# A dummy GpSimd write after every gather, and distances written in place of their comparison

## The chip, the cores and the metric

The kernel runs on one core of a Trainium2 chip. Times are device microseconds of that core for one launch; the time of a kernel is the median of several runs without the profiler. A profile is a separate execution of the same program under the hardware profiler, and its span can differ from the timed runs. Engines: PE (TensorE, matrix products; PEld are its weight loads), DVE (VectorE), ACT (ScalarE), POOL (GpSimd, which here issues indirect DMAs and little else), SP (SyncE, which issues the plain DMAs).

## What is computed

For each of 16 graphs with 1024 nodes and 64 channels: normalize and clip the node features, drop some neighbours by their rank in the adjacency row, take three quantiles per channel over the neighbours that remain, and put the weighted sum through a small two-layer network.

```python
h = jnp.maximum(_layernorm(x, axis=-1), 0.0)
# in the layer, x is h:
neigh = (adj_ > 0) & ~eye
rank = jnp.cumsum(ni, axis=-1) - ni                    # ni = neigh as integers
skip = jnp.where(nb > T, (nb + K - 1) // K, 1)         # nb = neighbours per node, T = 10, K = 2
rem = neigh & (sk > 1) & (rank % sk == sk - 1) & mask[:, :, None]
rem = rem | jnp.swapaxes(rem, 1, 2)
vals = jnp.where(nd[..., None], x[:, None, :, :], jnp.inf)   # nd: neighbours kept
s = jnp.sort(vals, axis=2)
for tau, w in zip((0.25, 0.5, 0.75), (0.25, 0.5, 0.25)):
    ...                                                # v_lo, v_hi: s at floor/ceil of tau * (nv - 1)
    agg = agg + w * (v_lo + frac * (v_hi - v_lo))
out = x + agg
y = jax.nn.relu(out @ W1 + b1) @ W2 + b2
```

## The kernel before

The kernel makes a list of neighbours per node, gathers their feature rows from a table in DRAM, and sorts the gathered rows with a fixed network. `drop` computes a distance `dist` (is this neighbour's rank one that is dropped?) and compares it; `keep` makes the remaining adjacency; `order` sorts the nodes by their number of neighbours (`perm`); `collect` packs the lists (`idx`). The tiles `rem` and `perm` share one buffer (tag `wide`, `bufs=1`).

```python
    def drop(b):
        ...
        rem = wk.tile([P, NT, N], BF16, name="rem", tag="wide", bufs=1)
        rems[b] = rem
        for t in range(NT):                                    # NT = 8
            dist = wk.tile([P, N], F16, name="dist")           # two buffers
            for n in range(2):
                rk = psum.tile([P, HALF], F32, name="rk", tag="mx", bufs=3)
                nc.tensor.matmul(rk, cnt[:, ts], ...)          # L702
                for s in range(4):
                    nc.tensor.matmul(rk[:, s * P:(s + 1) * P], ne[:, 4 * n + s, ts], upper, ...)   # L707
                nc.scalar.activation(dist[:, n * HALF:(n + 1) * HALF], rk, AF.Abs, bias=bias[:, t:t + 1])   # L711
            nc.vector.tensor_scalar(rem[:, t], dist, 1.0, half[:, t:t + 1], OP.add, OP.is_equal)   # L712
```

The gathers. A pair of batches has nodes in four classes by neighbours, each class with its own tile `g` (the first two, `g0` and `g1`, have two buffers, `g4` and `g6` one). Per batch there are 12 + 10 + 10 + 9 + 8 + 7 + 6 + 5 = 67 gathers, 1072 in all; each moves one row of 64 numbers to each of 128 partitions.

```python
CLASSES = (((0,), 13), ((1, 2, 3), 11), ((4, 5), 9), ((6, 7), 7))

    def fetch(m, classes=CLASSES, halves=(0, 1)):
        for tiles, slots in classes:
            lo, n = tiles[0], len(tiles)
            ...   # g = wk.tile(..., name=f"g{lo}", bufs=2 - lo // 4)
            for h in halves:
                nc.scalar.copy(g[:, slots - 1, :, h], owns[m][:, lo:lo + n, h])
                idx, tab = lists[2 * m + h], tables[2 * m + h]
                for k in tiles:
                    for s, slot in enumerate(order[:CAPS[k] - 1]):
                        at = PASSED[k] + s
                        nc.gpsimd.indirect_dma_start(          # L930
                            out=g[:, slot, k - lo, h], out_offset=None, in_=tab,
                            in_offset=bass.IndirectOffsetOnAxis(ap=idx[:, at:at + 1], axis=0),
                        )
```

`aggregate(m, o)` sorts and weighs a pair's tiles on VectorE (L961, L962 minima and maxima, L969 weights), first `g6` and `g4`, then asks for the next pair's `g4` and `g6`, then `g1` and `g0`. Nodes with many neighbours are treated in two groups of eight batches by `fetch_group` (L1100, 44 gathers, and L1104). The main loop weaves the preparation of the next pair between the results of this one:

```python
    for m in range(pairs + 1):                                 # pairs = 8
        if 0 < m < pairs:
            fetch(m, CLASSES[:1])
            ...                                                # a group's gathers, for two values of m
            fetch(m, CLASSES[1:2])
        ...
        side = chain(*(prepare(b) for b in (2 * m + 2, 2 * m + 3) if b < B))
        weave(chain(results(m - 1) if m else (), (1.0,)), 140.0 if m else 1.0, side, 85.0)
```

Instructions are placed on each engine's queue by a scheduler that respects the dependencies; `tc.keep_in_program_order` pins an instruction behind the one written before it on the same engine.

Of the kernel before, what the change touches and what calls it, by code (L numbers as in the profile page):

```python
# [28 lines left out]
F16 = mybir.dt.float16  # L29
BF16 = mybir.dt.bfloat16  # L30
FP8 = mybir.dt.float8e4
FP8W = mybir.dt.float8e5
I32 = mybir.dt.int32
# [6 lines left out]
P = 128  # L40
N = 1024
# [43 lines left out]
FP8_PARTS = (0, P, 2 * P, 3 * P, 4 * P, 4 * P + 17, 4 * P + 32)  # L85
# [449 lines left out]
def list_layer(  # L535
# [14 lines left out]
    nc = tc.nc  # L550
# [3 lines left out]
    cst = ctx.enter_context(tc.tile_pool(name="cst", bufs=1))  # L554
    wk = ctx.enter_context(tc.tile_pool(name="wk", bufs=2))
# [5 lines left out]
    def ask(b, t):  # L561
# [10 lines left out]
    ident16, ones16, minus16, before16, base, blocks, own2 = (  # L572
        kb[:, lo:hi] for lo, hi in zip(BF_PARTS, BF_PARTS[1:])
    )
    raw = wk.tile([P, FP8_PARTS[-1]], BF16, name="raw", tag="dist")
    nc.sync.dma_start(out=raw, in_=cbf[:, BF_AT:BF_AT + FP8_PARTS[-1]])
    rows_u8 = wk.tile([B * NT, P], U8, name="rows_u8", tag="rest", bufs=1)
    nc.sync.dma_start(out=rows_u8, in_=nodemask.rearrange("b (t p) -> (b t) p", p=P))
# [111 lines left out]
    def drop(b):  # L690

        ne = neT[b]
        bias, half = nbs[b]
        cnt = counts[b]
        rem = wk.tile([P, NT, N], BF16, name="rem", tag="wide", bufs=1)
        rems[b] = rem
        for t in range(NT):
            ts = slice(t * P, (t + 1) * P)
            dist = wk.tile([P, N], F16, name="dist")
            for n in range(2):  # L700
                rk = psum.tile([P, HALF], F32, name="rk", tag="mx", bufs=3)
                nc.tensor.matmul(  # L702
                    rk, cnt[:, ts], blocks[0:NT, 4 * n:4 * n + 4, None].to_broadcast([NT, 4, P]), start=True, stop=False,
                    skip_group_check=True,
                )
                for s in range(4):
                    nc.tensor.matmul(  # L707
                        rk[:, s * P:(s + 1) * P], ne[:, 4 * n + s, ts], upper, start=False, stop=(s == 3),
                        skip_group_check=True,
                    )  # L710
                nc.scalar.activation(dist[:, n * HALF:(n + 1) * HALF], rk, AF.Abs, bias=bias[:, t:t + 1])  # L711
            nc.vector.tensor_scalar(rem[:, t], dist, 1.0, half[:, t:t + 1], OP.add, OP.is_equal)  # L712
            yield 0.5
# [199 lines left out]
    pairs = B // 2  # L913
    gathered, groups = {}, {}

    def fetch(m, classes=CLASSES, halves=(0, 1)):

        for tiles, slots in classes:
            lo, n = tiles[0], len(tiles)
            held, order = PLANS[slots][:2]  # L920
            if (m, tiles) not in gathered:
                gathered[m, tiles] = wk.tile([P, held, n, 2, C], F32, name=f"g{lo}", bufs=2 - lo // 4)
            g = gathered[m, tiles]
# [7 lines that stand above are left out]
                            out=g[:, slot, k - lo, h], out_offset=None, in_=tab,  # L931
                            in_offset=bass.IndirectOffsetOnAxis(ap=idx[:, at:at + 1], axis=0),
                        )


    pause = cst.tile([P, 1], F32, name="pause")
# [61 lines left out]
    def aggregate(m, o):  # L998


        last = m == pairs - 1
        coef = coefs[m]
        for half in (0, 1) if last else (1, 0):
            acc = psum.tile([P, 4, 2, C], F32, name="acc", tag="agg", bufs=2)
            parts = CLASSES[2 * half:2 * half + 2][::1 if last else -1]
            for tiles, slots in parts:
                lo, n = tiles[0], len(tiles)
                nc.tensor.matmul(
                    acc[:, lo - 4 * half:lo - 4 * half + n], ident32, gathered[m, tiles][:, slots - 1],
                    start=((tiles, slots) == parts[0]), stop=False, skip_group_check=True,  # L1010
                )
            for tiles, slots in parts:
                lo, n = tiles[0], len(tiles)
                g = gathered.pop((m, tiles))
                plan = PLANS[slots]
                for k in tiles:
                    for slot in plan[1][CAPS[k] - 1:]:
                        nc.vector.memset(g[:, slot, k - lo], BIG)
                yield from sort(
                    g.rearrange("p s n h c -> p s (n h c)"), plan, window(tiles, slots)[0],  # L1020
                    lambda s, many: coef[:, s:s + many, lo:lo + n].rearrange("p s n h -> p s (n h)"),
                    acc[:, lo - 4 * half:lo - 4 * half + n],
                )
            if half and not last:
                fetch(m + 1, CLASSES[2:])
            terms(acc, [o[:, 4 * half:4 * half + 4, :, C * n:C * n + C] for n in range(3)])
# [145 lines left out]
    def prepare(b):  # L1172
        yield from both(drop(b), load(b + 1) if b + 1 < B else iter(()), normalize(b))
        yield from keep(b)
        yield from order(b)
        yield from collect(b)
# [28 lines left out]
    for _ in range(4):  # L1205
        next(ahead)
    late_constants()
    drain(both(ahead, drop(0), normalize(0)), keep(0), order(0), collect(0, ((0, 1), (1, NT))))
    fetch(0, halves=(0,))
    drain(load(1), prepare(1))  # L1210
    fetch(0, halves=(1,))
    for m in range(pairs + 1):
        if 0 < m < pairs:
# [92 lines left out]
@with_exitstack  # L1306
def quantile_graph_layer(
    ctx: ExitStack,
    tc: tile.TileContext,
    x: bass.AP,  # L1310
    adj: bass.AP,
    nodemask: bass.AP,
    W1: bass.AP,
    b1: bass.AP,
    W2: bass.AP,
    b2: bass.AP,
    cbf: bass.AP,
    cf32: bass.AP,
    ci32: bass.AP,
    out: bass.AP,  # L1320
):
    keep = ctx.enter_context(tc.tile_pool(name="keep", bufs=1))
    flag = keep.tile([1, 1], I32, name="flag")
    list_layer(tc, x, adj, nodemask, W1, b1, W2, b2, cbf, cf32, out, flag)
    full = tc.nc.values_load(flag[0:1, 0:1], min_val=0, max_val=1)
    with tc.If(full > 0):
        dense_layer(tc, x, adj, nodemask, W1, b1, W2, b2, cbf, cf32, ci32, out)
# [78 lines left out]
```

## Time and profile before

| | |
|---|---|
| time, median of 3 | 2034.06 us (2023.58 to 2036.27) |
| span under the profiler | 2713.0 us, mean granted TensorE clock 0.688 |
| gathers of `fetch` (L930) | 1072, mean 1.001 us each on POOL |
| sorting steps (L961, L962) | 408 each, 0.70 us each on DVE |
| `dist` (L711) | 256 on ACT, 0.69 us each |
| comparison (L712) | 128 on DVE, 0.49 us each |
| bytes moved | 130.12 MB, mean 48 GB/s over the profiled span |

A group of instructions in the profile is read as: line, engine, operation, tiles, count; busy time and mean of one; idle time of its engine just before, and what ended that idle time. "issue" is time in which an engine waited for nothing that the profile shows, "remote" or "an unknown queue" a wait whose end the profile can't assign to an instruction.

### The profile page before, as it was taken

The numbers are of one execution on the slowest core, as the hardware profiler recorded it, in microseconds if no ns is written. First come the engines' busy times: TensorE is split into PE (matmuls) and PEld (weight loads), VectorE is DVE, ScalarE is ACT, GpSimd is POOL, SyncE is SP. The second block draws the span as 40 slices with busy tenths as digits, with TensorE's granted clock in tenths as the row PEclk, the third lists the DMA queues.
The fourth block names the chain that finished last, engine by engine and source line by source line (L and its number), as shares of the span: only waits on it lengthen the run. The fifth ranks groups of instructions, "written<-read, shape, count | busy, mean of one in ns | idle before, by whom it ended". The sixth has DMA issues, their size and how long they took to land.

```text
span 2713.0 us, 25381 instructions
## 1 busy us (share of the span) xinstructions
PE 1377.2 (51%) x8367; PEld 737.9 (27%) x8385; DVE 1162.5 (43%) x3634; ACT 926.9 (34%) x2414; POOL 1128.6 (42%) x1129
## 2 busy tenths in 40 slices
PE   7227163433664655645564555643565665514435
PEld 3114132211332323322232333322332323202223
DVE  2202255232322752453523652466633554338692
ACT  6247243323552533243342544232341532100101
POOL 0630726353325454455525355445325345537100
PEclk7657576665776767766687767756677677656767
DMA  3232212021222231212212121222111211111000
GB/s 99 64 79 72 59 47 61 14 71 45 78 53 47 48 84 24 67 49 66 48 37 59 43 73 37 55 65 49 53 42 24 62 23 19 30 22 22 20 0 11
DMA packets 152591, 130.12 MB, mean 48 GB/s; under 512 B 117570, under 2 KB 118082, under 8 KB 152450
## 3 DMA queue, kind: packets, MB, share of 16 engines
q1 hardware_dynamic: 116482, 91.51, 12.1%
q0 software_dynamic: 35968, 36.90, 8.0%
q8 instruction: 68, 1.11, 0.2%
q14 instruction: 73, 0.60, 0.1%
HBM read 112.78 MB, written 13.81 MB: 47 GB/s over the span
## 4 chain that ended last, share of the span: by engine, by line
PE 37%; another core or an unknown queue 33%; issue 11%; ACT 10%; DVE 8%; DMA 1%; POOL 0%; SPq 0%; POOLq 0%; DVEq 0%; ACTq 0%
PE codeP L792 6%; PE rk L707 3%; PE acc L971 3%; PE rk L702 3%; PE kp L727 2%; PE kp L724 2%; ACT dist L711 2%; PE kp L723 2%; PE tp L646 2%; ACT sg L640 2%; PE low L1054 2%; PE high L1051 2%; PE cp L674 2%; DVE g L962 2%
## 5 line engine op out<-in xcount | busy, mean ns | idle before, releaser
L930 POOL DMA_INDIRECT g<-htab,idx x1072 | 1072.7, 1001 | 1324.7 <-issue 376.7
L646 PE MATMUL tp<-kb,sg 128*128 128x128 bf16 x1024 | 123.4, 270 | 400.6 <-issue 138.4
L961 DVE TENSOR_TENSOR g<-g 128x768 f32<-128x768 f32 (+3 forms) x408 | 279.5, 702 | 88.1 <-DMA g<-htab,idx 81.2
L962 DVE TENSOR_TENSOR g<-g 128x512 f32<-128x512 f32 (+3 forms) x408 | 279.3, 701 | 20.2 <-PE tp L651 10.7
L711 ACT ACTIVATE dist<-rk,bias 128x512 f16<-128x512 f32 x256 | 172.4, 690 | 329.2 <-remote 188.9
L712 DVE TENSOR_SCALAR rem<-dist,half 128x1024 bf16<-128x1024 f16 x128 | 62.8, 491 | 421.6 <-ACT dist L711 387.2
L656 ACT ACTIVATE ne<-tp 128x512 fp8e4<-128x512 f32 x240 | 136.3, 600 | 310.8 <-remote 214.2
L971 PE MATMUL acc<-g,kf 128*128 128x256 f32 (+2 forms) x448 | 155.0, 495 | 162.1 <-DVE g L969 120.4
L702 PE MATMUL rk<-kb,cnt 8*128 8x512 bf16 x256 | 126.0, 492 | 176.6 <-ACT dist L711 100.8
L646 PEld LDWEIGHTS <-sg 128*128 128x128 bf16 x1024 | 93.0, 123 | 428.8 <-issue 244.1
L792 PE MATMUL codeP<-pack,perm 128*128 128x332 bf16 x1024 | 201.3, 342 | 9.5 <-DVE pause L941 6.3
L728 ACT ACTIVATE kept<-kp 128x512 fp8e4<-128x512 f32 x256 | 151.8, 600 | 122.7 <-remote 87.9
L731 PE MATMUL code<-kw,kept 128*128 128x17 fp8e5 x1024 | 67.3, 175 | 172.3 <-ACT kept L728 95.7
L971 PEld LDWEIGHTS acc<-g,kf 128*128 128x128 f32 x448 | 96.3, 256 | 191.5 <-DVE g L969 125.6
L707 PEld LDWEIGHTS <-ne 128*128 128x128 fp8e4 x1024 | 75.1, 114 | 262.2 <-issue 261.3
L640 ACT ACTIVATE sg<-at 128x1024 bf16<-128x1024 f32 x128 | 132.6, 1055 | 13.3 <-DMA at<-in_adj_dram 13.3
L792 PEld LDWEIGHTS <-perm 128*128 128x128 bf16 x1024 | 95.9, 106 | 150.0 <-issue 84.3
L707 PE MATMUL rk<-kw,ne 128*128 128x128 fp8e5 x1024 | 131.6, 265 | 0.0
L805 DVE MAX8 keys<-codeP 128x8 f32<-128x128 f32 x128 | 38.0, 297 | 205.2 <-ACT own L800 128.6
L1032 DVE TENSOR_SCALAR at_p<-iota,node 128x512 bf16<-128x512 f16 x256 | 77.4, 360 | 111.3 <-remote 86.9
L795 ACT CAST st<-codeP 128x4 bf16<-128x4 f32 x128 | 21.4, 167 | 294.6 <-PE codeP L792 139.9
L727 PE MATMUL kp<-kw,rem 128*128 128x128 fp8e5 x1024 | 118.0, 239 | 0.0
(155 smaller groups left out, 2315.2 us busy)
## 6 DMA issues: line engine op xcount, KB each, us to landing
at<-in_adj_dram SPq DMA_DIRECT2D x128, 512.0 KB
g<-htab,idx POOLq DMA_INDIRECT x1072
xt<-in_x_dram SPq DMA_DIRECT2D x16, 256.0 KB
htab<-xt SPq DMA_DIRECT2D x16, 256.0 KB
gtab<-xt SPq DMA_DIRECT2D x16, 256.0 KB
y<-in_x_dram SPq DMA_DIRECT2D x16, 256.0 KB
out_dram<-y SPq DMA_DIRECT2D x16, 256.0 KB
gg<-g SPq DMA_DIRECT2D x16, 96.0 KB
```

The source lines that it names most:

```text
L640: nc.scalar.activation(sg, at, AF.Sign)
L646: nc.tensor.matmul(tp[:, s], sg[:, m * P:(m + 1) * P], ident16, start=(s == 0), stop=(s == 3 and t // 4 != n), skip_group_check=True,)
L702: nc.tensor.matmul(rk, cnt[:, ts], blocks[0:NT, 4 * n:4 * n + 4, None].to_broadcast([NT, 4, P]), start=True, stop=False, skip_group_check= ...
L707: nc.tensor.matmul(rk[:, s * P:(s + 1) * P], ne[:, 4 * n + s, ts], upper, start=False, stop=(s == 3), skip_group_check=True,)
L711: nc.scalar.activation(dist[:, n * HALF:(n + 1) * HALF], rk, AF.Abs, bias=bias[:, t:t + 1])
L727: nc.tensor.matmul(kp[:, s], rem[:, t, at:at + P], minus, start=False, stop=(s == 3))
L728: nc.scalar.activation(kept[:, 4 * n:4 * n + 4], kp, AF.Relu, saturate=False)
L792: nc.tensor.matmul(flat, perm[:, t, k * P:(k + 1) * P], pack[:, t], start=False, stop=(t == NT - 1))
L930: nc.gpsimd.indirect_dma_start(out=g[:, slot, k - lo, h], out_offset=None, in_=tab, in_offset=bass.IndirectOffsetOnAxis(ap=idx[:, at:at + ...
L961: nc.vector.tensor_tensor(at(f, df, n), pa, pb, one)
L962: nc.vector.tensor_tensor(pa if back else pb, pa, pb, other)
L971: nc.tensor.matmul(acc, ident32, lines[:, s], start=False, stop=(s == now[-1] and not ends), skip_group_check=True)
```

## The change

After each gather of `fetch`, GpSimd writes 256 numbers into a tile that nobody reads, so that gathers are further apart. The tile needs 1 KB of each partition; room is made by dropping the two `dist` buffers of 2 KB: ScalarE now writes a distance into the part of `rem` in which VectorE then puts the comparison's result. `raw`, a tile of the start that used a `dist` buffer, uses one of `sg`'s.

```diff
-    raw = wk.tile([P, FP8_PARTS[-1]], BF16, name="raw", tag="dist")
+    raw = wk.tile([P, FP8_PARTS[-1]], BF16, name="raw", tag="sg")
...
         for t in range(NT):
             ts = slice(t * P, (t + 1) * P)
-            dist = wk.tile([P, N], F16, name="dist")
+            dist = rem[:, t].bitcast(F16)
...
+    spent = cst.tile([P, 256], I32, name="spent")
+
+    def delay():
+        tc.keep_in_program_order(nc.gpsimd.iota(spent, pattern=[[1, 256]], base=0, channel_multiplier=0))
+
     def fetch(m, classes=CLASSES, halves=(0, 1)):
...
                             in_offset=bass.IndirectOffsetOnAxis(ap=idx[:, at:at + 1], axis=0),
                         )
+                        delay()
```

## The prediction

> **What bounds the kernel now.** I read the page's head first: 2034.06 us is the median of the timed runs, but the execution under the profiler took 2713.0 us. So the first question is which 679 us of the profile the timed run doesn't have. The page's busy times and its chain of waits:
>
> ```profile
> span 2713.0 us, 25381 instructions
> PE 1377.2 (51%) x8367; PEld 737.9 (27%) x8385; DVE 1162.5 (43%) x3634; ACT 926.9 (34%) x2414; POOL 1128.6 (42%) x1129
> ...
> PE 37%; another core or an unknown queue 33%; issue 11%; ACT 10%; DVE 8%; DMA 1%; POOL 0%; SPq 0%; POOLq 0%; DVEq 0%; ACTq 0%
> ```
>
> No engine is full, and a third of the chain is waiting for "an unknown queue", on a program of one core. Busy times of single stretches show when that happens. Columns: stretch, length, busy (count) of PE, PEld, DVE, ACT, POOL, granted TensorE clock, DMA share, GB/s:
>
> ```profile
> 1056.00:1110.00 54.00, 47.81 (x339) 24.71 (x341) 23.25 (x123) 34.08 (x115) 0.00 (x0) 0.91 0.14 36
> 1110.00:1163.00 53.00, 17.70 (x83) 8.77 (x82) 11.88 (x30) 7.07 (x12) 39.98 (x41) 0.64 0.25 55
> ```
>
> With no gather PE runs 339 matmuls in 54 us; in the next 53 us, in which GpSimd issues 41 gathers, it runs 83, and ScalarE and VectorE also stop. Instructions in order of time show it closer (start, length, engine, line, [idle before]):
>
> ```profile
> 1358.96 0.38 PE L1054 MATMUL low<-at_p,o 128*64 128x512 bf16 x1
> 1358.99 0.95 POOL L930 DMA_INDIRECT g<-htab,idx  x1 [0.30 <-issue]
> 1360.24 0.94 POOL L930 DMA_INDIRECT g<-htab,idx  x1 [0.30 <-issue]
> ...
> 1375.24 0.95 POOL L930 DMA_INDIRECT g<-htab,idx  x1 [0.30 <-issue]
> 1381.25 0.58 ACT L1058 COPY lows<-low 64x512 f32<-64x512 f32 x1 [12.02 <-remote]
> 1381.25 0.88 DVE L1032 TENSOR_SCALAR at_p<-iota,node 128x512 bf16<-128x512 f16 x3 [32.45 <-remote]
> ```
>
> PE's last matmul of `low` starts at 1358.96, and its two readers start together at 1381.25, a few us after the last gather of the burst. Meanwhile GpSimd alone works, one gather every 1.25 us (0.95 busy, 0.30 gap).
>
> I added up the stretches of over 3 us in which PE, VectorE and ScalarE are all idle: about 680 us, nearly all inside bursts of gathers. 2713 - 680 = 2033, which is the timed median. The simplest reading is that these stops belong to the profiled execution[...] and the timed run has none. That is an inference; it decides the sign of the prediction.
>
> If it holds, GpSimd's account in the timed run is: 1072 gathers x 1.25 = 1340 us, plus 44 group gathers x (1.05 + 0.30) = 59 us and 8 others of about 1.3, together 1410 us of 2034. The first gather starts at 81 us; the last ends at 2518 of 2713, leaving a tail of 195. So between first and last gather the timed run has 2034 - 81 - 195 = 1758 us, of which GpSimd works 1410 and waits about 350. It is the fullest engine of that stretch. VectorE already waits for it:
>
> ```profile
> DVE g L961 <- DMA g<-htab,idx: 81.2, 11, 30.9
> ```
>
> (total us, times, longest), and that is in the profile, where the other engines are held back and GpSimd is not.
>
> [...]
>
> **The change part by part.** (1) The iotas. `delay()` is called once per gather of `fetch`: 1072 times; the 44 + 4 group gathers get none. The price comes from the two ends that the trace has:
>
> ```profile
> L583 POOL IOTA iota_i<- 128x1024 int32 x1 | 1.0, 972 | 0.4 <-POOLq L1395 0.4
> ...
> L1395 POOL MEMSET const-float32-0.0<- 128x1 f32 x1 | 0.1, 100 | 0.3 <-issue 0.3
> ```
>
> 1024 numbers take 972 ns and one number 100 ns, so (972 - 100) / 1023 = 0.85 ns per number, and 256 numbers take 100 + 218 = 318 ns. The gap of 0.30 us behind a gather should stay; behind the iota there may be none or another up to 0.30. I take 0.04, as light GpSimd instructions follow each other closely at the start: 0.36 us each, 1072 x 0.36 = 386 us in all (limits 0.32 to 0.62: 343 to 665). GpSimd's cycle goes from 1.25 to 1.61 us, a pair of batches from 134 x 1.25 = 168 us to 216.
>
> How much of the 386 fits into the idle 350? The first stretch of idleness (165 to 275 us in the profile, GpSimd waiting for batch 1's list, about 59 us of the burst before it being stopped compute, so some 50 us in the timed run) can't be used: each gather needs its list. Nor can the tail wholly: the last gathers feed the last sorts. Work 1410 + 386 = 1796, + 81 head + 50 + 195 tail = 2122 with no other idleness; if the tail can shrink to 100 (the last sorts and the last two outputs), 2027. Of the other 300 us of waits (for lists, and for `g4` and `g6`, which have one buffer) I expect a quarter to a third to remain, some 80 to 100. That gives 2027 + 90 = 2117 to 2122 + 90 = 2212. I choose 2155.
>
> (2) `dist` in `rem`'s memory. ScalarE no longer waits for one of two `dist` buffers. What the trace of `dist` has to say (lines L711, L712, and ScalarE's waits for the comparison):
>
> ```profile
> L711 ACT ACTIVATE dist<-rk,bias x256: 667/687/730, 21.2 to 2239.2; 128x512 f16<-128x512 f32 x128
> L712 DVE TENSOR_SCALAR rem<-dist,half x128: 467/486/709, 23.1 to 2239.9; 128x1024 bf16<-128x1024 f16 x128
> ...
>   DVE rem L712: 7.1, 4
> ```
>
> The wait removed is 7.1 us in four cases. In its place, the first `dist` of a batch must now wait until the one buffer `wide` is free, so until the previous batch's last `codeP` matmul has read `perm`. Before, two tiles could be made ahead: 2 x 2 x 0.687 = 2.7 us of ScalarE per batch, 16 x 2.7 = 44 us at most, and most of it beside other work. I put it at +10, between -7 and +44. The comparison in place reads and writes the same 2-byte forms, so its 486 ns should stay. `raw` moving to `sg`'s buffers touches only the start: 0 to 5 us.
>
> Sum: 2155 + 10, less some 5 for VectorE doing more while GpSimd spaces itself out: 2160.
>
> **The rivals.** *The stops are real.* If the timed run also stops in bursts, spacing gathers by 29% (1.61 for 1.25) may[...] shorten every stop. For it: the change has no other visible purpose. Against it: then 2713 - 2034 would have to come from somewhere else, and single instructions in the profile are not stretched (matmuls of 512 columns at 0.22 us apart, gathers at 0.94 to 0.95). It would give 1900 to 2000. *GpSimd has more room than I think.* If the 0.30 gap or a part of the 0.95 is the profiler's, or the iota runs inside the gap, then 1072 x 0.1 to 0.2 = 107 to 214 us go into 350 us of waits and the time stays at 2030 to 2080. For it: no timed run shows the cycle. *GpSimd becomes the bound outright.* With two gaps, 0.62 x 1072 = 665 us: 1410 + 665 + 81 + 50 + 100 to 195 = 2306 to 2401. For it: every one of the 1034 gaps behind a gather is 0.30, whatever the gather's length. *The order changes.* The iotas write one tile, so they form a chain in program order, while gathers are placed when their list is ready; iotas may bunch behind the second list's gathers. This shifts delays, not their sum; some tens of us either way.
>
> **Range and chances.** The middle is 2160; the first two rivals set the low end, the third the high end: 1990 to 2340. Faster by over 2% (below 1993) needs the stops to be real: 0.15. Within 2% (to 2075) needs over four fifths of the iotas to be hidden: 0.18. Slower by over 2%: 0.67.
>
> **What the changed profile would show.** Right: iotas of about 0.32 us, gathers 1.55 to 1.7 us apart, GpSimd busy about 1128 + 341 = 1470 us, longer bursts, more time in VectorE's wait for the gathers, `dist` waits at most some tens of us different. The profiled span may fall while the timed one rises[...]. Wrong: a timed run below 1993, which would mean that the stops exist without the profiler; gathers still 1.25 apart; or iotas that cost far from 0.32.

## The result, and the profile after

| | before | changed |
|---|---|---|
| time, median | 2030.88 us (2023.58 to 2036.27) | 2215.24 us (2213.13 to 2217.07) |
| ratio | | 1.091, 95% interval 1.087 to 1.095 |
| profiled span | 2713.0 us, in a second profile 2028.6 us | 2212.4 us |

The change makes the kernel 9.1% slower, some 184 us. The lines of the changed kernel's page that answer to those shown of before:

```profile
span 2212.4 us, 26445 instructions
PE 1314.6 (59%) x8385; PEld 715.4 (32%) x8385; DVE 1196.1 (54%) x3634; ACT 920.5 (42%) x2414; POOL 1558.9 (70%) x2201
...
POOL 0584857788768887888888878883668878886000
...
PE 36%; POOL 34%; DVE 13%; issue 8%; ACT 6%; DMA 3%; SPq 0%; POOLq 0%; DVEq 0%; ACTq 0%
```

GpSimd is the fullest engine and holds 34% of the chain of waits, where it held 0% in the first profile. "An unknown queue", 33% there, is gone, but it is also gone from a second profile of the kernel before (e1), so the change did not remove it. The third line is GpSimd's busy share in 40 slices: mostly 7 to 8 tenths from the seventh slice to the end of the gathers, then three empty slices in which VectorE sorts the last pair.

GpSimd's groups (line, engine, operation, count, busy, mean ns, idle before). Line numbers of the changed kernel are 7 higher behind the new function; L936 is the gather that was L930:

```profile
L936 POOL DMA_INDIRECT g<-htab,idx x1072 | 1115.0, 1040 | 434.0 <-issue 205.8 <-DVE idx L834 170.3 <-DVE pause L948 33.6
L920 POOL IOTA spent<- 128x256 int32 x1072 | 387.5, 361 | 24.9
```

And in order of time:

```profile
946.73 0.94 POOL L936 DMA_INDIRECT g<-htab,idx  x1 [0.16 <-issue]
947.68 0.35 POOL L920 IOTA spent<- 128x256 int32 x1
948.20 0.94 POOL L936 DMA_INDIRECT g<-htab,idx  x1 [0.16 <-issue]
949.15 0.36 POOL L920 IOTA spent<- 128x256 int32 x1
949.67 0.94 POOL L936 DMA_INDIRECT g<-htab,idx  x1 [0.16 <-issue]
```

An iota starts as its gather ends, and the next gather starts 0.16 us after the iota. Gathers are 1.47 us apart instead of 1.25.

VectorE waits for the gathers (total us, times, longest), 526 us in all, where it waited 369 before (e1):

```profile
DVE g L968 <- DMA g<-htab,idx: 525.7, 33, 75.5
```

### The profile page after: what moved, and what is told of

Its sections match the earlier page's. It is cut to its first block, busy times and chain, and to the rows that moved or that the text cites. A ratio compares the mean times of both kernels' runs of the same rounds, so it can differ in the third digit from the quotient of the medians.

```text
span 2212.4 us, 26445 instructions
## 1 busy us (share of the span) xinstructions
PE 1314.6 (59%) x8385; PEld 715.4 (32%) x8385; DVE 1196.1 (54%) x3634; ACT 920.5 (42%) x2414; POOL 1558.9 (70%) x2201
## 4 chain that ended last, share of the span: by engine, by line
PE 36%; POOL 34%; DVE 13%; issue 8%; ACT 6%; DMA 3%; SPq 0%; POOLq 0%; DVEq 0%; ACTq 0%
POOL g L936 24%; POOL spent L920 8%; PE codeP L792 8%; DVE g L968 3%; PE acc L978 3%; DVE g L969 3%; PE rk L707 2%; PE rk L702 2%; PE cp L674 2%; PE kp L727 2%; PE kp L724 2%; PE kp L723 2%; PE low L1061 2%; PE high L1058 2%; PE tp L646 2%
## 5 line engine op out<-in xcount | busy, mean ns | idle before, releaser
L936 POOL DMA_INDIRECT g<-htab,idx x1072 | 1115.0, 1040 | 434.0 <-issue 205.8
L968 DVE TENSOR_TENSOR g<-g 128x512 f32<-128x512 f32 (+3 forms) x408 | 279.6, 700 | 538.8 <-DMA g<-htab,idx 525.7
L920 POOL IOTA spent<- 128x256 int32 x1072 | 387.5, 361 | 24.9
L969 DVE TENSOR_TENSOR g<-g 128x512 f32<-128x512 f32 (+3 forms) x408 | 279.0, 701 | 2.3 <-DMA gg<-g 0.8
L711 ACT ACTIVATE rem<-rk,bias 128x512 f16<-128x512 f32 x256 | 170.4, 695 | 140.7 <-PE rk L707 138.2
L646 PE MATMUL tp<-kb,sg 128*128 128x128 bf16 x1024 | 116.0, 265 | 110.4 <-ACT sg L640 105.4
L724 PE MATMUL kp<-rem,kw 128*128 128x512 bf16 x256 | 102.2, 400 | 102.6 <-DVE pause L948 68.5
L727 PEld LDWEIGHTS <-rem 128*128 128x128 bf16 x1024 | 82.6, 101 | 149.4 <-issue 112.1
L1058 PE MATMUL high<-at_p,o 128*128 128x512 bf16 x256 | 76.9, 412 | 83.1 <-DVE at_p L1039 83.1
L712 DVE TENSOR_SCALAR rem<-rem,half 128x1024 bf16<-128x1024 f16 x128 | 68.0, 531 | 98.5 <-ACT rem L711 98.2
L990 ACT CAST o<-acc 128x512 bf16<-128x512 f32 x48 | 28.0, 583 | 212.3 <-PE acc L978 198.2
```

Of the source, the lines that this page charges most:

```text
L646: nc.tensor.matmul(tp[:, s], sg[:, m * P:(m + 1) * P], ident16, start=(s == 0), stop=(s == 3 and t // 4 != n), skip_group_check=True,)
L724: nc.tensor.matmul(kp, minus, rem[:, 4 * n:4 * n + 4, ts], start=False, stop=False)
L920: tc.keep_in_program_order(nc.gpsimd.iota(spent, pattern=[[1, 256]], base=0, channel_multiplier=0))
L936: nc.gpsimd.indirect_dma_start(out=g[:, slot, k - lo, h], out_offset=None, in_=tab, in_offset=bass.IndirectOffsetOnAxis(ap=idx[:, at:at + ...
L968: nc.vector.tensor_tensor(at(f, df, n), pa, pb, one)
L969: nc.vector.tensor_tensor(pa if back else pb, pa, pb, other)
```

## The experiments

For each kernel I added up GpSimd's occupied time from its instructions in order of time: gathers of both kinds, scattered rows and iotas, with gaps under 1 us counted in. The table is sorted by it. "Over" is the time over the kernel with distances in place and no iotas (2042.5).

| run | iotas | occupied | time, us | over | over / added occupied |
|---|---|---|---|---|---|
| e6, 112 gathers fewer | none | 1364 | 1949.8 | -93 | 0.69 |
| e1, before again | none | 1498 | 2031.2 | | |
| e2, distances in place | none | 1498 | 2042.5 | 0 | |
| e3 | 1072 of 1 number | 1573 | 2082.7 | 40 | 0.54 |
| e7, late | 416 of 256 | 1623 | 2102.7 | 60 | 0.48 |
| e11, late | 416 of 240 | 1628 | 2103.6 | 61 | 0.47 |
| e8, early | 656 of 256 | 1655 | 2200.8 | 158 | 1.01 |
| e10, early | 656 of 240 | 1656 | 2171.7 | 129 | 0.82 |
| e12, two chains | 1072 of 256 | 1784 | 2214.7 | 172 | 0.60 |
| e9 | 1072 of 240 | 1801 | 2216.2 | 174 | 0.57 |
| the change | 1072 of 256 | 1809 | 2215.2 | 173 | 0.56 |
| e4, bunched | 1072 of 256 | 1833 | 2222.8 | 180 | 0.54 |
| e5 | 1072 of 512 | 2014 | 2347.2 | 305 | 0.59 |

**e1: the kernel before, profiled again.** No edit.

> The kernel before, unchanged, to see whether its long profiled span comes again. If the stops of all engines during bursts of gathers belong to being profiled: timed 2030 +-15 and a profiled span of 2600 to 2800 again. If the 2713 us of the first profile was one odd execution: a profiled span near 2030.

Measured: 2031.15 us, ratio 0.9998 (0.9976 to 1.0021), and a profiled span of 2028.6 us. The long span did not come again. The same stretch of it in time (columns as in the prediction's table of stretches):

```profile
1056.00:1110.00 54.00, 42.66 (x278) 23.48 (x278) 50.01 (x126) 31.00 (x73) 38.04 (x34) 0.87 0.34 94
1110.00:1163.00 53.00, 42.88 (x313) 24.58 (x312) 43.29 (x147) 34.80 (x97) 41.12 (x40) 0.87 0.35 85
```

With 40 gathers in 53 us PE runs 313 matmuls, where it ran 83 beside 41 gathers. So the first profile of before showed one odd execution, whose cause stays open. From here on the kernel before is read from this second profile, whose span agrees with the timed runs. Its page, as far as it answers to the lines shown above:

```profile
span 2028.6 us, 25381 instructions
PE 1286.1 (63%) x8367; PEld 708.5 (35%) x8385; DVE 1166.9 (58%) x3634; ACT 914.4 (45%) x2414; POOL 1160.9 (57%) x1129
...
POOL 0272662777165777577747775772657777771000
```

A part of the stops remains. I count 17 stretches of over 3 us in which PE, VectorE and ScalarE are all idle, together 231 us (670 in the first profile, 365 with the change). The gathers, and VectorE's wait for them:

```profile
L930 POOL DMA_INDIRECT g<-htab,idx x1072 | 1107.3, 1033 | 656.8 <-issue 315.7 <-DVE idx L834 166.1 <-DVE at_p L1032 76.1
```

```profile
DVE g L961 <- DMA g<-htab,idx: 369.4, 30, 42.6
```

Before the change VectorE already waits 369 us for gathers (81 in the first profile), and GpSimd is occupied for 1498 us of 2029. Its idle time between first and last gather is 256 us. Of the 166 us that the profile calls a wait for `idx`, 80 lie before the first gather, and other pauses carry other names. In order of time, though, each of the ten pauses of over 1 us before a gather (80 us before the first one, 253 us later) ends 0.3 to 0.7 us after VectorE has finished a batch's list. One that the profile puts down to `at_p`:

```profile
631.60 0.26 DVE L834 SCALAR_TENSOR_TENSOR idx<-bit,low 128x104 int32<-128x104 f32 x1
...
632.13 1.07 POOL L930 DMA_INDIRECT g<-htab,idx  x1 [15.36 <-DVE at_p L1032]
```

So GpSimd's idle time is the wait for lists.

**e2: distances in place, no iotas.** The tile `spent` goes too.

```diff
-                        delay()
```

> Distances written in place of the comparison, no iotas. Theory (the cost is GpSimd's time for 1072 iotas): 2010 to 2060, no more than 30 us from the kernel before, and a profiled span with the stops, 2550 to 2800. Rival (the first distance of a batch waits for the single wide buffer, and that is what costs): 2080 to 2200.

Measured: 2042.51 us, ratio to before 1.0047 (1.0029 to 1.0064). Without iotas the kernel is 10 us slower than before; the rival of 2080 to 2200 is out. Its comparison (VectorE) beside that of before from e1:

```profile
L712 DVE TENSOR_SCALAR rem<-rem,half 128x1024 bf16<-128x1024 f16 x128 | 64.5, 505 | 91.5 <-ACT rem L711 91.1
```

```profile
L712 DVE TENSOR_SCALAR rem<-dist,half 128x1024 bf16<-128x1024 f16 x128 | 63.9, 500 | 72.6 <-ACT dist L711 66.8 <-PE codeP L792 5.5
```

Reading and writing the same bytes cost next to nothing here (505 for 500 ns); what changed is that VectorE waits 91 instead of 67 us for ScalarE, which can no longer make two distances ahead. In e1 the first distance of a batch (from the third batch on) starts 16 to 46 us before the previous batch's last `codeP` matmul ends, in e2 always 0.35 us after it. That some of these 24 us make up the 10 is not shown apart: VectorE's and ScalarE's instructions also came into another order. No profiled span above the timed one here either, so that part of the expectation failed together with e1's.

**e3: iotas of one number.**

```diff
-    spent = cst.tile([P, 256], I32, name="spent")
+    spent = cst.tile([P, 1], I32, name="spent")
-        ... pattern=[[1, 256]] ...
+        ... pattern=[[1, 1]] ...
```

> The changed kernel with 1 number per iota in place of 256. In the changed profile a gather is followed by its iota with no gap, and by the next gather after 0.16 us; with an iota of 0.10 us the cycle would be 0.94 + 0.10 + 0.16 = 1.20 us, as long as before (1.25). Theory (GpSimd's time): 2000 to 2060. Rival (the chain of 1072 pinned iotas forces a worse order on all engines): 2120 to 2220. If gathers 1.2 us apart are what stops the engines under the profiler, its profiled span is 2500 or more although it has the iotas.

Measured: 2082.67 us, ratio 1.0244 (1.0194 to 1.0295), 23 us above the theory's range and below the rival's. GpSimd's iotas:

```profile
L920 POOL IOTA spent<- 128x1 int32 x1072 | 157.0, 146 | 29.9
```

An iota of one number takes 146 ns, not 100. Behind a gather that is nearly free: 0 + 0.146 + 0.16 takes the place of a gap of 0.30. But not every iota stands behind its own gather. The iotas write one tile and so stay in program order, while gathers are placed as lists come ready; iotas pile up:

```profile
999.46 0.95 POOL L936 DMA_INDIRECT g<-htab,idx  x1 [0.16 <-issue]
1000.43 4.48 POOL L920 IOTA spent<- 128x1 int32 x23
1005.58 1.25 POOL L936 DMA_INDIRECT g<-htab,idx  x1 [0.67 <-DVE g L968]
1007.14 1.09 POOL L936 DMA_INDIRECT g<-htab,idx  x1 [0.30 <-issue]
```

The 23 in a row take 4.48 us, 0.19 us each, and the gathers that lost theirs keep their gap of 0.30. Occupied time rises by 75 us, and the time by 40 over e2. That fits GpSimd's time as the cause, with 1 us of it showing as 0.54; how much of the 40 us comes from the changed order alone, this run can't say.

**e4: the same iotas, bunched.**

```diff
                 for k in tiles:
                     for s, slot in enumerate(order[:CAPS[k] - 1]):
                         ...                                    # the gather
-                        delay()
+                for k in tiles:
+                    for _ in order[:CAPS[k] - 1]:
+                        delay()
```

> The same 1072 iotas of 256 numbers, but behind the gathers of a class and half instead of between them; gathers run back to back. Theory (GpSimd's total time): 2180 to 2240, like the changed kernel's 2215. Rival (the pace of single gathers matters, not the total): near 2030 to 2100. Under the profiler the stops should be back with gathers 1.25 us apart, so a profiled span clearly above the timed one, 2350 or more.

Measured: 2222.80 us, ratio 1.0929 (1.0874 to 1.0983). The edit did not give what its name says. The scheduler put many iotas between later gathers, and in the trace 552 of the 1072 gathers still have an iota right behind them (799 in the changed kernel):

```profile
961.33 0.94 POOL L936 DMA_INDIRECT g<-htab,idx  x1 [0.16 <-issue]
962.27 0.37 POOL L920 IOTA spent<- 128x256 int32 x1
962.80 0.94 POOL L936 DMA_INDIRECT g<-htab,idx  x1 [0.16 <-PE tp L651]
```

498 gathers instead of 258 are followed at once by the next gather, and the time doesn't fall. That speaks for GpSimd's total and against the distance of single gathers, but gathers without any iota between them were not run beside the same total. (The profiled span, 2223.7, is not above the timed one.)

**e5: twice the numbers.**

```diff
-    spent = cst.tile([P, 256], I32, name="spent")
+    spent = cst.tile([P, 512], I32, name="spent")
-        ... pattern=[[1, 256]] ...
+        ... pattern=[[1, 512]] ...
```

> Twice the numbers. From the iotas of 1 and of 256 numbers (146 and 361 ns) one of 512 should take 577 ns: 1072 x 0.216 = 231 us more of GpSimd than in the changed kernel. So far 0.54 to 0.56 of each us added to GpSimd has shown in the time. If that share is constant: 2215 + 127 = 2342. If it was so low only because GpSimd had idle time left to fill (144 us between first and last gather in the changed kernel, some of it not usable), the share rises towards one: 2390 to 2446.

Measured: 2347.23 us, ratio 1.1575 (1.1527 to 1.1622), an iota of 582 ns. The time is near the 2342 of a constant share, but by two errors that cancel: 205 us of occupied GpSimd came on top (2014 - 1809), not 231, and 132 us of time, so the share of this step is 0.64 instead of 0.55. GpSimd's idle time from first to last gather falls to 85 us (256 before, 144 with the change), so there was still slack to fill, and the jump to a share of one did not come.

**e6: fewer gathers, no iotas.** To e2, one gather fewer for seven of eight node tiles; VectorE fills the slot with the large number. The kernel leaves out one neighbour of some nodes.

```diff
-                    for s, slot in enumerate(order[:CAPS[k] - 1]):
+                    for s, slot in enumerate(order[:CAPS[k] - 1 - (k > 0)]):
...
-                    for slot in plan[1][CAPS[k] - 1:]:
+                    for slot in plan[1][CAPS[k] - 1 - (k > 0):]:
```

> No iotas; distances in place; in seven of the eight node tiles of a batch the last gather is left out and its slot filled with the large number by VectorE, so one neighbour of some nodes is missing from the result. 112 gathers of 1.34 us fewer: 150 us less of GpSimd, 112 small VectorE writes more (19 us at 165 ns). If GpSimd bounds the kernel without iotas too, with the same share of 0.54: 2042 - 81 = 1961, at most 2042 - 150 = 1892. If it doesn't, and the iotas only made it so: 2030 to 2065.

Measured: 1949.82 us, ratio to before 0.9621 (0.9587 to 0.9655). The slope goes on below the kernel before: 135 us less of GpSimd, 93 us less time, although VectorE has 56 writes more (3690 instructions for 3634; not the 112 expected, as one write fills the slot of both batches of a pair). The gathers that remain are as far apart as before (1.25 us), so it is their number that counts. So gathers already bound the kernel before the change; the iotas did not make a new bound.

**e7 and e8: only a part of the iotas.** e7 has those behind the gathers into `g4` and `g6` (one buffer each), e8 those into `g0` and `g1` (two buffers each).

```diff
-                        delay()
+                        if lo >= 4:                             # e8: if lo < 4
+                            delay()
```

> Iotas of 256 numbers only behind the gathers into the two tiles with a single buffer, g4 and g6: 416 of the 1072, about 416 x 0.29 = 121 us of GpSimd. If only GpSimd's total counts: 2042 + 0.55 x 121 = 2109 (2090 to 2130). If the wait for the single buffers is the chain: the whole 121, so 2150 to 2170.

> The other 656 iotas, behind the gathers into the double-buffered g0 and g1: about 656 x 0.29 = 190 us of GpSimd. If only the total counts: 2042 + 0.55 x 190 = 2147 (2125 to 2170), and this and the run with the other 416 add up to the changed kernel's 173 us over the kernel with distances in place. If the single buffers are the chain: at most 2070.

Measured: e7 2102.71 us, ratio 1.0389 (1.0354 to 1.0424), e8 2200.77, ratio 1.0871 (1.0834 to 1.0909). e7 falls in the range of "only the total counts". e8 doesn't: its 157 us show whole, and the parts add up to 218, not to 173. The single buffers are not the chain, since their iotas are the cheaper ones. But the total alone isn't the whole story. The pauses before gathers, from the first gather on, show where the difference lies: 270 us in e2, 209 in e7, 272 in e8. In e7 iotas fill pauses, in e8 they fill none.

**e9 to e12: the same work in another order.** A small edit of the iota's size can change the order that the scheduler finds; two tiles in place of one, chosen by batch, make two chains of iotas.

```diff
-    spent = cst.tile([P, 256], I32, name="spent")
+    spent = cst.tile([P, 240], I32, name="spent")               # e9, e10 (if lo < 4), e11 (if lo >= 4)
+    spent = [cst.tile([P, 256], I32, name=f"spent{n}") for n in range(2)]      # e12, delay(h)
```

> All 1072 iotas, 240 numbers in place of 256: 1072 x 16 x 0.84 ns = 14 us less of GpSimd. If GpSimd's total sets the time: 2215 - 8 = 2207 (2200 to 2215). If the order that the scheduler happens to find is worth as much as the iotas: off by 30 us or more, up or down.

> The 656 early iotas with 240 numbers. They cost 158 us of time for 157 us of GpSimd with 256 numbers, where the total alone would have given 86. Theory 1, early gathers lie on the chain, the place of an iota matters: 2201 - 5 to 9 = 2190 to 2198. Theory 2, that run had an unlucky order: with another order (the schedule of VectorE changes in many places by this small edit) the time comes down to 2110 to 2160.

> The 416 late iotas with 240 numbers, a schedule nearly that of the run with 256: 2103 - 3 = 2100 (2090 to 2106) under every theory; it shows how far the time follows such a small edit when the order stays.

> All 1072 iotas of 256 numbers, but those of the two batches of a pair write two different tiles, so they are two chains and fall into other places of GpSimd's queue. GpSimd's work is the changed kernel's. If only the total counts: 2215 +-15. If the bunching of iotas behind the second batch's gathers is part of the cost: 2140 to 2190, or above 2240 where the new order is worse.

Measured: e9 2216.18, ratio 1.0911 (1.0862 to 1.0960); e10 2171.66, 1.0702 (1.0654 to 1.0749); e11 2103.59, 1.0368 (1.0313 to 1.0424); e12 2214.73, 1.0913 (1.0865 to 1.0960). With all iotas in place the time hardly moves (2215 to 2216), but the order hardly moved either: in e9 it is nearly the changed kernel's on every engine, in e12 only GpSimd's differs much. e9 lies 1 us above its theory's range of 2200 to 2215. In e10 the order of VectorE and ScalarE did change, and the early iotas alone moved by 29 us for an estimated 9 us of iota time (656 x 16 x 0.84 ns), between both theories: part of e8's excess was its order. The trace shows where. e8 makes the list of batch 8 (the first of its pair) late:

```profile
1057.45 0.26 DVE L834 SCALAR_TENSOR_TENSOR idx<-bit,low 128x104 int32<-128x104 f32 x1
...
1058.44 1.75 POOL L936 DMA_INDIRECT g<-htab,idx  x1 [33.15 <-issue]
```

In e10 that list is finished at 954.4 us and this pause does not exist; all pauses together are 240 us, for 272 in e8. At a share of 0.82 the early iotas are still dearer than the late ones at 0.47. Why is not settled. What fits is that early gathers of the second batch start only when its list is ready, and everything that follows for this pair waits behind them; that was not tried by itself.

No version with iotas beats the kernel before, and no kernel that computes the whole result was found that does; e6 shows that fewer gathers would.

## Why the prediction was right

**The sign and the inference behind it.** The sign was right, and so was the step that carried it: the first profile is no picture of the timed run. The reason given, that the stops belong to being profiled, was wrong: no later profile has a span above its timed runs. Nor has the timed run none of them, since the second profile, as long as a timed run, still has 231 us. So 2713 - 680 = 2033 hit the median by luck: taking away only what the first profile has more than the second (670 - 231 = 439 us) would have given 2274, not 2031. The stops that remain lie where GpSimd issues gathers while the other engines have nothing to do, and the change made them longer (365 us).

**GpSimd's account.** Predicted: 1410 us occupied, some 350 idle, tail 195. Measured in e1: 1498, 256 and 194. The gather's mean cycle was taken from its median (1.25); with the means of e1 it is 1.033 + 0.30 = 1.33. The difference, 1072 x 0.08 = 86 us, is about the 88 that were missing. Nor was "every one of the 1034 gaps" 0.30: the waits of the first profile have one of 22.3 us among them.

**The price of an iota.** Predicted 318 ns plus 0.04 of gap (at the start of the first profile GpSimd's four memsets begin 0.03 us apart), 386 us in all. Measured 361 ns, 311 us of occupied time. The two errors have opposite signs: an iota of one number takes 146 ns (e3), not the 100 of the first profile's memset, while the gap behind a gather did not stay. It went from 0.30 to 0.16: an iota starts as its gather ends (947.68 for 946.73 + 0.94), and 0.16 us pass between it and the next gather. Where an iota stands behind its gather the cycle grew by 1.47 - 1.25 = 0.22 us; the mean over all 1072 is 311 / 1072 = 0.29, since the bunched ones save no gap. "The order changes" was the rival that expected some to bunch, and they did. The 0.85 ns per number held: (361 - 146) / 255 = 0.84 ns from the iotas of 1 and 256 numbers, and (582 - 361) / 256 = 0.86 ns from those of 256 and 512.

**How much is hidden.** This is the mis-sized term. Predicted: 386 added, some 260 of it hidden in idle time, 126 shown. Measured: 311 added; idle time between first and last gather fell from 256 to 144, the last wait, before the last rows are scattered, from 184 to 172, the head by 3; 311 - 112 - 12 - 3 = 184, the whole difference. Only 127 us were hidden. The prediction let two thirds of the waits fill; in fact under half did, because GpSimd waits for lists, and these come later too. With the change 220 of the 222 us of pauses before gathers (78 of them before the first) end within 2 us after a list is finished, as all 333 did before, and the last list is finished at 1815 us instead of 1669. VectorE makes the lists, and its own waits for gathers go from 369 to 526 us. The reading that fits both is that a longer burst of gathers delays the lists that the next bursts need. So 2160 was 55 us too low: 75 us too much added, 133 too much hidden, and a base of 2031 instead of 2034. That the first two have opposite signs is luck: with the iotas priced right and the same 260 us hidden, the prediction would have been about 2085. The choice of 2155 within 2117 to 2212 rested on an estimate of the waits that no line showed.

**The in-place distances.** Predicted +10 (between -7 and +44); e2 has +10. The lost two tiles ahead show in its trace, as the prediction said; that they make up the whole 10 us is not shown.

**The rivals.** That the timed run stops as much as the first profile, and that spacing gathers shortens the stops, is out by e1 and by the result. More room on GpSimd is out by the measured account. GpSimd as an outright bound, every us showing, is not reached even with 512 numbers.

**VectorE's comparisons beside the iotas.** The prediction took 5 us off for VectorE; instead its two-byte comparisons (`TENSOR_SCALAR`) became longer. `at_p`, `perm` and the dropped-neighbour comparison take 370, 482 and 505 ns without iotas (e2), 424, 514 and 531 with 256 numbers, and 477, 651 and 564 with 512. Without iotas (e2), then with 512 numbers (e5):

```profile
L1035 DVE TENSOR_SCALAR at_p<-iota,node 128x512 bf16<-128x512 f16 x256 | 80.1, 370 | 17.7 <-PE low L1057 17.6
L769 DVE TENSOR_SCALAR perm<-iota,place_f 128x1024 bf16<-128x1024 f16 x128 | 52.8, 482 | 0.0
...
L1039 DVE TENSOR_SCALAR at_p<-iota,node 128x512 bf16<-128x512 f16 x256 | 108.2, 477 | 13.2 <-PE low L1061 13.1
L769 DVE TENSOR_SCALAR perm<-iota,place_f 128x1024 bf16<-128x1024 f16 x128 | 74.8, 651 | 0.0
L712 DVE TENSOR_SCALAR rem<-rem,half 128x1024 bf16<-128x1024 f16 x128 | 72.0, 564 | 97.8 <-ACT rem L711 97.6
```

In e5 the 69 `perm` instructions that overlap an iota take 800 ns in the mean, the other 59 take 477, about as long as without iotas (482). In the changed kernel the lengthening adds 14 + 4 + 4 = 22 us to VectorE's busy time. The sorting steps, float32 with two inputs, stay at 700 ns (704 before, 703 and 701 in e5). Why a comparison takes longer beside an iota and the sorting steps don't, no run here shows. How much of the 22 us reaches the time was not measured apart.

**Left open.** The granted TensorE clock was 0.735 in the changed kernel's profile and 0.761 in e1, and PE was busy for 1314.6 us instead of 1286.1. Whether a part of the 184 us comes from that was not tested.

## What to carry to other kernels

Before reading a profile, compare its span with the timed runs: if they differ by a third, find what differs or profile again, and judge an engine by its occupied time (busy plus the short gaps between its instructions, here 0.16 and 0.30 us) in the timed span. An engine that is 74% occupied (1498 of 2031) can already be the bound where its instructions wait for lists that depend on its own earlier results: here 0.47 to 0.82 of each us added or taken away showed in the time, and in one order of the instructions (e8) all of it. Idle time hides added work only as far as inputs are there early enough: here 127 of 311 us. Which input a pause waits for is safer read from what was finished just before it ended than from the name that a profile gives it.

## What the runs showed that was not expected

- An iota of one number behind a gather cost little: it takes 0.146 us (e3) and the gap before the next gather shrinks to 0.16, together 0.31 us in place of a gap of 0.30.
- The median gather cycle (1.25 us) is 0.08 below the mean (1.33): not every gather takes the usual 0.95 us; in the first profile single ones take up to 1.9.
- An edit of 16 numbers per iota moved the time by 1 us where the order of the instructions stayed nearly the same (e7 to e11, the changed kernel to e9), and by 29 us where VectorE's and ScalarE's order changed (e8 to e10).
